# Layer 2's weight preparation moved beside an idle engine, two samples' norms moved into the spectra, and the output stage issued in a listed order

## The chip, the cores and the metric

The kernel runs on one NeuronCore of a Trainium2 chip. Five engines matter: TensorE (PE, matrix products; PEld are its weight loads), VectorE (DVE), ScalarE (ACT), GpSimd (POOL) and SyncE (SP), which here only issues DMA transfers. Each takes its own list of instructions in order and waits on semaphores for the others. The metric is the device time of one execution in microseconds (us). The profile is one execution seen by the hardware profiler.

## The reference, cut to what matters

The input is x of shape (4, 56, 56, 128) in float32. Four layers follow, each as x = x + layer(group_norm(x)):

```python
# layer 0: attention in shifted 7x7 windows, then attention over all 3136 positions, then an MLP
# layer 1: edge features relu(x_i W1 + x_j W2), summed over j; a node matrix
# layer 2: a spectral ("neural operator") attention block over 56x56 images, 128 images a sample
#   xa_n = _inorm(xa, norm_g[0], norm_b[0])
#   k, q, v = _fno_layer(xa_n, wK..), _fno_layer(xa_n, wQ..), _fno_layer(xa_n, wV..)   # FFT products
#   attn_w = softmax(q k^T / sqrt(d)); out = attn_w v
#   projd = _fno_layer(out, wP..); attention = _inorm(projd + xa); an = _inorm(attention)
#   m = _fno_layer(an, wM0.., gelu); m = _fno_layer(m, wM1..); return _inorm(m) + attention
# layer 3: relu of a 3-tap convolution with row and column sums, plus x
```

Three things are concerned here. First, layer 2 needs for each sample the group norm and the image norm of layer 1's result ("norms"), before its Fourier transforms ("spectra"). Second, two tables that depend on the weights alone: one for the scores (from wQ and wK) and one for the values (from wV and wP). Third, everything from the projection to the end ("the output stage").

## The kernel before: the parts that the change and the steps touch

The samples go one after the other through layers 0 and 1. Within a sample the order is 7x7 windows, attention over all positions, MLP, edge layer. The norms of sample b-1 for layer 2 are steps of a generator that the window code of sample b interleaves with its own work (`beside`):

```python
def norms(b, bank):
    if b < 0:
        return iter(())
    return normed_images(k, w2, st, b, io, bank, x1w, xad[b])

for b in range(B):                       # B = 4 samples
    first_layers(lambda *a: fast_attention(*a, functools.partial(norms, b - 1), k.mr[:, b, :]), I["x"][b],
                 x2d[b] if b < B - 1 else None, loaded=b == 0)
```

The norm of one sample, cut (every `yield` ends a step):

```python
def normed_images(k, w, st, b, wk, bank, xp, xad):
    for t in range(HH):                              # HH = 56
        nc.vector.bn_stats(rows[:, t, :], x[:, t, :])
        if t % 2 == 1:
            yield
    nc.vector.bn_aggr(mv, ...)
    ...                # a chain of small DVE operations, four small matmuls and one ACT square root
    for t in range(0, HH, 14):
        apply_norm(k, x[:, t:t + 14, :], x[:, t:t + 14, :], mr)       # DVE, in place
        if t == 42:
            nc.sync.dma_start(xad, x)                # the normed image goes to memory
    ...                # ACT root, DVE reciprocal and scale: st.norm[:, b, 1, :]
```

Between the layers, the images are loaded back, and the spectra stage starts. PE, ACT and DVE follow the order of the program there (`manual_schedule`):

```python
def images(b):
    if b not in loaded:
        xp = loaded[b] = x2p.tile([P, HH + 1, HH], F32, name="s_x2")
        for t in range(0, HH, 28):
            nc.sync.dma_start(xp[:, t:t + 28, :], xad[b, :, t:t + 28, :])
        ...
for b in range(2):
    images(b)
nc.sync.dma_start(x2d[B - 1], x1)
...                                                  # loads of layer 3's and of the convolution weights
with tc.tile_pool(name="g_wk", bufs=1, side="right") as wk:
    all_score_weights(k, I, w2, sp, wk, st)          # POOL alone
    value_weights(k, I, w2, wk, dd)                  # POOL alone
    spectra(k, w2, st, xad, images)

def spectra(k, w, st, xad, images):
    ...
    norm = normed_images(k, w, st, B - 1, wk, ..., st.x1, xad[B - 1])
    first = [first_transform(k, st, b, (wk, psum), st.x1 if b == B - 1 else images(b), zs) for b in range(B)]
    for _ in first[0]:
        pass
    for b in range(B):
        for n, _ in enumerate(sample_spectra(k, st, b, (wk, psum), zs.pop(b))):   # 13 steps
            for _ in range(3):
                next(norm, None)
            if b < B - 1 and n in (2, 5, 7, 9):
                next(first[b + 1])

def first_transform(k, st, b, pools, x, to):         # 4 steps
    for t0 in range(0, HH, 14):
        for t in range(14):
            for ri in range(2):
                nc.tensor.matmul(ps[...], xf[...], k.fw[:, ri, :], start=True, stop=True)   # s_pr
        nc.vector.tensor_mul(z[:, :, t0:t0 + 14], ps..., bc(st.norm[:, b, 1, t0:t0 + 14], 1, 33))
        nc.scalar.copy(z[:, :, HH + t0:...], z[:, :, t0:t0 + 14])
        yield
```

`sample_spectra` takes `z` through further products (`s_ps`, a second `s_pr`, eight groups `s_px`), whose results ACT and DVE copy out. The weight tables are built by some 55 POOL operations of up to 128x512 elements.

The output stage is a plan of 788 operations: 40 for two groups of attended rows and 187 for each sample, two half samples and the last layer. Each is a short group of instructions of one engine, with a list of operations that must come before it and the buffers that it takes and gives back. Before, a list scheduler with estimated costs chose the order:

```python
class Plan:
    HOP, SETS = 0.25, 1.3
    def issue(self):
        while left:
            best = None
            for op in left:
                ...            # the earliest start t by estimated costs, dependences and free buffers
                if t is not None and (best is None or t < best[0] - 1e-9):
                    best = t, op
            op.run()
            free[op.engine] = op.end = t + op.cost
            ...
```

The operations of a half sample follow one chain: `over_h` (PE, 14 matmuls, L1883), `over_c` (PE, L1900), `over_w` (PE, L1914), `product` (PE, L1936), then DVE and POOL combine, ACT squares, `sums` (PE, L1967), a root, and again, three times over. The last layer of a sample has four `convolve` operations (PE, L2317, 12 matmuls each or 6), which need nothing of the other samples.

## Time and profile before

| quantity | value |
|---|---|
| time, median of 3 (lowest, highest) | 3878.21 us (3872.31, 3882.3) |
| span of the profiled execution | 3873.3 us |
| busy share PE, DVE, ACT, POOL | 92%, 75%, 54%, 31% |
| mean granted PE clock | 0.958 |
| spectra: first transform to first score product | 2888.7 to 2977.5 us |
| output stage, after the last mixing products | about 3476 to 3873.3 us |

How to read it: PE is busy nearly everywhere, so the sum of busy times does not say where something can be gained. One goes by stages. A table by stretches of time gives for each stretch its length, each engine's busy time with the number of instructions, and the PE clock that was granted. Where PE is busy for less than the stretch, or its clock is under 1, something other than the number of products sets the time. Waits are read engine by engine: the time that an engine stood idle, and what it stood for.

The four passes through layers 0 and 1 take about 700 us each and are the larger part of the span. Of these, the change touches only the 7x7 windows.

### The profile page before, as it was taken

What the parts mean: (1) busy time and instruction counts of PE and PEld (TensorE: products, weight loads), DVE (VectorE), ACT (ScalarE), POOL (GpSimd) and SP (SyncE); (2) the same over time, 40 slices, a digit from 0 to 9 for tenths busy, and PEclk for the clock granted to TensorE, in tenths of its full rate; (3) what the DMA queues carried; (4) which work ended last, traced back from release to release, by engine and by line L of the source; (5) the groups of instructions that cost most, each with busy time, mean ns of one, the idle gap of its engine ahead of it and who ended that gap; (6) DMA issues with size and microseconds to landing.
All of it is one profiled execution on the core that took longest, in us unless ns stands there. A gap on an engine that the chain in (4) does not pass through costs nothing. (4 is left out here: it accounts for less than half of the span.)

```text
span 3873.3 us, 79430 instructions
## 1 busy us (share of the span) xinstructions
PE 3546.0 (92%) x35416; PEld 1589.1 (41%) x35416; DVE 2897.3 (75%) x2703; ACT 2077.8 (54%) x2080; POOL 1210.6 (31%) x667
## 2 busy tenths in 40 slices
PE   6899999989998998999989989999998989989988
PEld 4422234543322455322245532223456433336654
DVE  6588877859887786688869758887776767765664
ACT  4577765448776554677745457776542012214332
POOL 0000006600000570000028300000655769975555
PEclk8999999999999999999999999999998989998888
DMA  2000000000000000000000000000011058831101
GB/s 96 1 1 1 1 1 19 19 18 1 1 1 1 18 3 34 1 1 1 1 17 3 19 18 1 1 1 34 2 44 49 1 121 170 175 101 59 52 8 50
DMA packets 73496, 111.12 MB, mean 29 GB/s; under 512 B 62140, under 2 KB 63932, under 8 KB 67900
## 3 DMA queue, kind: packets, MB, share of 16 engines
q1 hardware_dynamic: 14460, 93.13, 8.0%
q10 hardware_dynamic: 58688, 12.85, 2.0%
q8 instruction: 279, 4.57, 0.5%
q14 instruction: 69, 0.57, 0.0%
HBM read 79.46 MB, written 26.51 MB: 27 GB/s over the span
## 5 line engine op out<-in xcount | busy, mean ns | idle before, releaser
L663 ACT ACTIVATE f_ring<-f_s 128x1792 f32<-128x1792 f32 (+3 forms) x796 | 1097.3, 1429 | 226.6 <-PE f_s L661 224.8
L606 DVE TENSOR_TENSOR f_acc<-f_acc,f_ring 128x1792 f32<-128x1792 f32 x560 | 1134.1, 2025 | 64.3 <-ACT f_ring L663 7.5
L661 PE MATMUL f_s<-f_qT,f_kT 32*128 32x448 f32 x5376 | 738.3, 572 | 47.9 <-ACT f_ring L663 27.9
L877 POOL TENSOR_TENSOR m_sq<-m_y 128x392 f32<-128x392 f32 x16 | 14.5, 919 | 1975.4 <-ACT m_y L876 1975.3
L612 PE MATMUL f_po<-f_ring,f_va 128*32 128x448 f32 x5376 | 589.8, 546 | 0.0
L1029 DVE TENSOR_TENSOR e_td<-e_pa,e_c 128x1792 f32<-128x1792 f32 x252 | 491.3, 2013 | 14.4 <-ACT e_a L994 14.4
L1031 POOL TENSOR_TENSOR e_tp<-e_a,e_c 128x1792 f32<-128x1792 f32 x140 | 451.8, 3257 | 145.1 <-PE e_acc L1036 104.4
L661 PEld LDWEIGHTS f_s<-f_qT,f_kT 32*128 32x128 f32 x5376 | 268.4, 183 | 524.5 <-ACT f_ring L663 378.9
L1036 PE MATMUL e_acc<-e_td,t_shared 32*32 32x448 f32 x8064 | 323.7, 546 | 22.0 <-DVE e_td L1029 10.9
L1033 ACT ACTIVATE e_tp<-e_tp 128x1792 f32<-128x1792 f32 x140 | 235.1, 1696 | 176.2 <-POOL e_tp L1031 176.2
L1645 DVE TENSOR_TENSOR u_ud<-u_px,u_d 112x1792 f32<-112x1792 f32 x144 | 240.1, 1708 | 96.4 <-PE u_po L1650 87.3
L612 PEld LDWEIGHTS f_po<-f_ring,f_va 128*32 128x32 f32 x5376 | 133.2, 109 | 396.3 <-issue 395.3
L1036 PE MATMUL e_acc<-e_tp,t_shared 32*32 32x448 f32 x4480 | 222.3, 547 | 3.2 <-ACT e_tp L1033 2.5
L1650 PE MATMUL u_po<-u_ud,AT 112*64 112x448 f32 x960 | 201.6, 550 | 23.3 <-DVE u_ud L1645 23.3
L1647 POOL TENSOR_TENSOR u_up<-xh,u_d 112x1792 f32<-112x1792 f32 x64 | 193.8, 3054 | 25.7 <-PE u_po L1650 12.4
L1036 PEld LDWEIGHTS e_acc<-e_td,t_shared 32*32 32x32 f32 x8064 | 134.1, 103 | 146.4 <-DVE e_td L1029 56.0
L629 DVE RECIPROCAL f_den<-f_den 128x448 f32<-128x448 f32 x28 | 82.7, 2953 | 77.2 <-ACT f_den L628 77.2
L1650 PE MATMUL u_po<-u_up,AT 112*64 112x448 f32 x576 | 126.9, 548 | 0.2
L1650 PEld LDWEIGHTS u_po<-u_ud,AT 112*64 112x64 f32 x960 | 64.9, 137 | 147.9 <-issue 86.7
L606 DVE TENSOR_TENSOR f_acc<-f_ring 128x1792 f32<-128x1792 f32 x28 | 56.7, 2025 | 86.6 <-ACT f_ring L663 57.7
L1512 POOL TENSOR_TENSOR q_u<-iS,q_g 128x1792 f32<-128x1792 f32 x32 | 102.7, 3237 | 56.2 <-PE s_px L1360 33.4
L1036 PEld LDWEIGHTS e_acc<-e_tp,t_shared 32*32 32x32 f32 x4480 | 95.2, 103 | 55.3 <-ACT e_tp L1033 19.4
(485 smaller groups left out, 4797.0 us busy)
## 6 DMA issues: line engine op xcount, KB each, us to landing
u_d<-dd SPq DMA_DIRECT2D x48, 784.0 KB
xw<-in_x SPq DMA_DIRECT2D x4, 1568.0 KB
x2d<-x SPq DMA_DIRECT2D x4, 1568.0 KB
xad<-x SPq DMA_DIRECT2D x4, 1568.0 KB
x_xs<-xad ACTq DMA_DIRECT2D x32, 196.0 KB
xm<-x_ev ACTq DMA_DIRECT2D x64, 98.0 KB
o_a<-xm SPq DMA_DIRECT2D x8, 784.0 KB
o_x<-x2d SPq DMA_DIRECT2D x4, 1568.0 KB
```

What stands on the lines that cost most here:

```text
L606: nc.vector.tensor_add(acc, slots(j, 0) if c == 1 else acc, slots(j, c))
L612: nc.tensor.matmul(po[heads[h], :NB], va[o, c, heads[h]], p, start=(c == 0), stop=(c == 24))
L661: nc.tensor.matmul(ss[:, i, :NB], kT[heads[h], c * P:(c + 1) * P], qT[heads[h], blk(j)], start=True, stop=True)
L663: nc.scalar.activation(ring[:, slot:slot + m, :], ss[:, :m, :NB], AF.Exp, scale=scale)
L1029: nc.vector.tensor_tensor(t, am, cm, ALU.max)
L1031: nc.gpsimd.tensor_sub(t, bc(a.rearrange("p (l n) -> p l n", l=8), 1, 4), cm)
L1033: nc.scalar.activation(tf, tf, AF.Relu)
L1036: nc.tensor.matmul(acc[quarters[q], r, :NB], k.ident[o, o], t[o, q].rearrange("p l n -> p (l n)"), start=(g == 0), stop=(g == len(EDGE_TUR ...
L1512: nc.gpsimd.tensor_mul(u, bc(st.iS[:, bp, c, :HH], 1, HEADS), bc(g[:, n, c, :], 2, HH))
L1645: nc.vector.tensor_mul(u, bc(px[:, :, :NB], 2, m), dm)
L1647: nc.gpsimd.tensor_mul(u, bc(x, 2, m), dm)
L1650: nc.tensor.matmul(po[64 * b2:64 * b2 + 64, :NB], st.AT[:, 8 * i + h0 + q, 2 * bp + b2, :], u[:, b2, q, :], start=(left == 16), stop=(left ...
```

## The change

It has two parts. The first moves work between stages:

- The weight tables of layer 2 are built beside sample 0's 7x7 windows, where POOL has only memsets to do. Their results go to memory (`gd`, `dd`), and `g` is loaded back before the spectra.
- Only sample 0's norms stay beside windows (the windows of sample 1). The norms of samples 1 and 2 move from the windows of samples 2 and 3 into the spectra, where before only sample 3's norms were. The spectra take the samples in the order 0, 3, 1, 2, and load samples 1 and 2 as they came from layer 1 (`x2d`), not normed (`xad`).

```diff
@@ spectra
-        norm = normed_images(k, w, st, B - 1, wk, ..., st.x1, xad[B - 1])
+        order = [0, B - 1, *range(1, B - 1)]
+        def steps(n):
+            for norm in norms[:1]:
+                for _ in range(n):
+                    if next(norm, norm) is norm:
+                        norms.pop(0)
+                        break
+        norms = [normed_images(k, w, st, b, wk, ..., of(b), xad[b]) for b in order[1:]]
...
         for _ in first[0]:
-            pass
-        for b in range(B):
+            steps(3)
+        for i, b in enumerate(order):
             for n, _ in enumerate(sample_spectra(k, st, b, (wk, psum), zs.pop(b))):
-                for _ in range(3):
-                    next(norm, None)
-                if b < B - 1 and n in (2, 5, 7, 9):
-                    next(first[b + 1])
+                if i < B - 1 and 8 <= n < 12:
+                    while n == 8 and len(norms) + i >= B - 1:
+                        steps(1)
+                    next(first[i + 1])
+                steps(4)
@@ all_score_weights
-    st.g = pool.tile([P, 2, 16, HEADS], F32, name="q_g")
-    st.g4 = pool.tile([P, 2, 1, HEADS], F32, name="q_g4")
+    g = wk.tile([P, 2, 17, HEADS], F32, name="q_g")
...
+    nc.sync.dma_start(gd, g)
@@ value_weights
-    nc.gpsimd.tensor_copy(f[:, 0], d[:, 0])
...                      # the three results are written from d and w.V, without the copy
@@ build
+            def layer2_weights():
+                ...      # all_score_weights(.., gd), then value_weights(.., dd)
             def norms(b, bank):
-                if b < 0:
+                if b == 0:
+                    layer2_weights()
+                if b != 1:
                     return iter(())
-                return normed_images(k, w2, st, b, io, bank, x1w, xad[b])
+                return normed_images(k, w2, st, 0, io, bank, x1w, xad[0])
...
-                    nc.sync.dma_start(xp[:, t:t + 28, :], xad[b, :, t:t + 28, :])
+                    nc.sync.dma_start(xp[:, t:t + 28, :], (x2d if b else xad)[b, :, t:t + 28, :])
...
+                g = sp.tile([P, 2, 17, HEADS], F32, name="g")
+                nc.sync.dma_start(g, gd)
+                st.g, st.g4 = g[:, :, :16], g[:, :, 16:]
+                spectra(k, w2, st, xad, images)
```

The second part replaces the list scheduler of the output stage by a fixed list of the 788 operations, which a search has found. The operations, their dependences and their buffers are the same:

```diff
-    def issue(self):
-        ...              # list scheduling by estimated costs
+    def issue(self, order):
+        assert sorted(order) == list(range(len(self.ops)))
+        ...
+        for n in order:
+            op = self.ops[n]
+            ...
+            op.run()
...
+OUTPUT_ORDER = """
+0 40 119 227 306 10 3 2 1 4 5 13 12 11 14 15 6 9 7 8 18 19 16 17 41 228 120 42 307 121 43 45 44 122 124 229 47
...
+781 782 785 786 787
+"""
-        plan.issue()
+        plan.issue([int(n) for n in OUTPUT_ORDER.split()])
```

## The prediction, as it was put on record before the run

> **What bounds the kernel now.** I read the page first: PE 92% busy, clock 0.958, so the average shows no single spare place and one has to go by stages. Next a table by stretches: the 7x7 windows of the four samples, the spectra, the output stage. (Columns: length; busy us and instructions of PE, PEld, DVE, ACT, POOL; granted PE clock; DMA share; GB/s.)

> ```profile
> 55.20:155.10 99.90, 91.01 (x728) 55.65 (x728) 52.61 (x100) 47.64 (x80) 6.85 (x18) 0.94 0.00 1
> 755.10:865.00 109.90, 94.77 (x732) 57.13 (x732) 66.52 (x181) 48.12 (x82) 6.80 (x18) 0.92 0.07 28
> 1465.10:1575.00 109.90, 94.76 (x732) 57.12 (x733) 66.51 (x181) 48.14 (x82) 6.79 (x18) 0.92 0.07 28
> 2178.50:2288.40 109.90, 94.85 (x732) 57.24 (x732) 66.60 (x181) 48.13 (x82) 6.86 (x18) 0.92 0.07 28
> 2888.50:2977.50 89.00, 73.31 (x1208) 64.04 (x1208) 50.70 (x133) 32.94 (x72) 39.24 (x58) 0.88 0.28 97
> 3476.00:3873.30 397.30, 353.89 (x2202) 233.34 (x2200) 225.47 (x393) 144.65 (x203) 221.45 (x132) 0.85 0.12 45
> ```

> Sample 0's windows carry no norm and take 99.9 us; the others carry one and take 109.9. So a norm beside windows costs 10.0 us, though DVE is far from full: its operations stand in DVE's queue ahead of the copies that PE waits for.

> In the spectra POOL's weight tables run beside sample 3's norm. DVE's timeline shows operations on one element per partition that take over 1 us next to others of 0.15:

> ```profile
> 2917.72 0.15 DVE L1764 TENSOR_TENSOR factors<-factors,t_w_ms 128x1 f32<-128x1 f32 x1
> 2918.51 0.94 DVE L1255 TENSOR_TENSOR s_t<-s_mv,s_mr 128x1 f32<-128x1 f32 x1
> 2919.49 1.18 DVE L1256 SCALAR_TENSOR_TENSOR s_t<-s_t,s_mv 128x1 f32<-128x1 f32 x1
> 2930.58 4.62 DVE L193 TENSOR_SCALAR x<-x,s_mr 128x784 f32<-128x784 f32 x4
> ```

> PE's timeline of the same stretch, in brackets the idle time and what ended it:

> ```profile
> 2912.17 0.38 PE L1250 MATMUL s_pt<-s_mv,t_shared 128*128 128x1 f32 x2 [3.49 <-DVE s_mv L1247]
> 2920.73 0.58 PE L1259 MATMUL s_pt<-s_t,t_shared 128*128 128x1 f32 x2 [3.83 <-DVE s_t L1256]
> 2926.20 0.68 PE L1283 MATMUL s_pt<-s_mean,c_ones_c 128*128 128x56 f32 x2 [1.72 <-DVE s_mean L1279]
> 2929.73 0.67 PE L1292 MATMUL s_pt<-s_sq,c_ones_px 128*128 128x56 f32 x2 [2.43 <-DVE s_sq L1289]
> ```

> From 2908 to 2933 PE does little, waiting for one norm; after it a sample takes 16.6 us (2933.3, 2950.0, 2966.6), bound by PE. In the output stage PE is busy 353.9 of 397.3 us at a clock of 0.85: idle time and clock cost about 43 and, at 15% of 354, some 53 us. Its waits have many causes and no main one:

> ```profile
> PE o_b L1967 <- ACT o_t L1956: 9.1, 4, 6.5
> PE o_d L1900 <- POOL o_v L2159: 6.3, 4, 3.6
> PE o_b L1967 <- ACT o_sq L2019: 3.9, 1, 3.9
> PE o_d L1883 <- ACT o_y L2034: 2.9, 1, 2.9
> ```

> [...] L1256 took 1.18 us beside POOL operations of 1.2 us, 0.22 us beside an idle POOL; the scaling of a 128x784 piece took 1.15 us against 0.68. [...]

> **The change, part by part.**

> *a. Windows of samples 2 and 3.* They lose their norms: 2 x (109.9 - 99.9) = 20.0 us off a path on which nothing else is parallel. **-20.**

> *b. Windows of sample 0.* They gain about 50 POOL operations, in the spectra some 33 us of POOL. Their loads (1.2 MB) begin near 53 us, when memory is idle; at the 420 GB/s that the image loads reached they need 3 us and are there before POOL ends its memsets at 62. Up to 16 normalisations wait on average half a POOL operation, 0.6 us, two groups ahead of use. I put **+1**.

> *c. Start of the spectra.* Before, SP issued the image loads at 2673, long ahead. In the built program after, the load of `g` stands before them on SP and waits for the edge layer's last matmul, since its buffer lies where the edge layer works (e_td). The images then wait too. From 2887.6: issue and start 1.2 us, `g` (0.56 MB) 1.3, the first image (1.6 MB) 3.8 at 420 GB/s, of which half must be there: first product near 2893 instead of 2888.7, **+4.5**. DVE loses it as well, its first operation being the copy-out.

> *d. First norm in the spectra (sample 3).* Its chain, from the aggregate to the norm, took 24.3 us (2912.1 to 2936.4). Without POOL I take off 7 us of excess in the chain and 5.5 in the convolution-weight operations (L1750 to L1768) between: about 12 to 15. **-10.**

> *e. Two more norms in the spectra.* In the program's order a sample is: four rounds of first transform and `s_px` (1.82 + 0.97 us on PE, so 11 us), with 24 `bn_stats` hidden beside; then 32 more at 0.123 us (3.9), the aggregate 1.67, and the chain: operations 8.7 us, four trips to PE and one to ACT 3. PE starts on the first scaled quarter, about 2 us before the chain ends. Sum 11 + 3.9 + 1.7 + 11.7 - 2 = 26.3 us a sample against 16.6. Twice: +19.4. The first sample's own 32 odd `bn_stats`, of which before 30 lay beside products, and PE at a lower clock in these gaps add some 9. **+28.**

> Spectra: 4.5 - 10 + 28 = about +23. First part: -20 + 1 + 23 = **+4**.

> *f. Output stage.* Same operations, same buffers, so only idle time and clock can change. I compared both orders on PE. A PE operation that needs the result of an earlier PE operation through another engine, with no other PE operation between, stands still for the whole detour; there are 12 such pairs before and 4 after (with at most one between: 33 and 29). Before, sample 3 ends with half 1 alone: nine of the twelve lie among PE's operations 155 to 185, and there the trace has 3.65, 3.91, 1.44, 1.33 and 1.28 us of idle PE. After, both halves of sample 3 alternate to the end, and the last layer's means stand before sample 2's last convolve. Some 8 detours of 2 us are filled: -16. What stays: the first product waits for the attended rows (2.87 us), the end after the last product (some 7 us). The clock should gain a few us, and a list found for estimated durations loses a few on the chip. **-18, between -45 and +5.**

> Sum: 3878.2 - 20 + 1 + 23 - 18 = **3864 us**.

> **The rivals.** *Spectra costs nothing.* If the norms fill PE's gaps, as the step counts intend, the stage stays near 89 us. For it: DVE was busy only 50.7 us there, and the POOL contention goes. Against it: the norm is a chain, a sample's first product needs its end, and three chains now follow one another with PE starved. Then the time would be near 3842. *POOL's tables disturb sample 0's windows.* If DVE's small operations there suffer as in the spectra (7 us in a chain of 24), sample 0 loses 5 to 10 us: 3870. [...] *The order yields nothing.* PE was 89% busy in the output stage, and the clock, not the idle time, may be the larger loss; a different mixture of small matmuls can lower it. Then 3880 to 3890. *The order yields much.* If the filled gaps also keep the clock at 0.92, 7% of 354 us come on top: 3840.

> **Range and chances.** The two parts nearly cancel in my sum and each has an error of about 15 us; together some 22. The range is 3834 to 3894. For 2% the time must fall under 3800.6 or rise over 3955.8. The first needs the favourable rival in the spectra and 45 us from the order; the second has no mechanism that I can see. Faster 0.03, within 2% 0.95, slower 0.02.

> **What would show it.** a: windows of samples 2 and 3 at 100 us. b: sample 0's at 101, POOL busy from 62 to about 100 us. c: PE idle for 4 to 5 us after the edge layer's last product, ended by a DMA. d: L1256 at 0.2 us and the 128x784 scalings at 0.7. e: the spectra at 105 to 115 us, three gaps of about 12 us in which PE waits for DVE's s_mv, s_t, s_mean and s_sq. f: output stage at 375 to 385 us, with fewer idle gaps after 3800. The prediction is wrong if the spectra stay under 95 us, or if the output stage changes by over 45 us or by nothing.

## The result, and the profile after

The changed kernel takes 3833.43 us (median of 4 runs, 3827.72 to 3834.5) against 3878.43 us (4 runs, 3872.31 to 3882.3): 0.9882 of the time, 95% interval 0.9865 to 0.9900. Predicted were 3864 us and a range of 3834 to 3894, so the sum was -14 where -45 was measured. Two lines of the profiled run's page (its span is 3825.9 us):

```profile
PE 3515.6 (92%) x35416; PEld 1573.8 (41%) x35416; DVE 2884.8 (75%) x2703; ACT 2078.0 (54%) x2080; POOL 1209.1 (32%) x666
PEclk9999999999999999999999999999997989999999
```

TensorE is busy for 92% of the span as before, with as many instructions, but for 3515.6 us instead of 3546.0. The same work became shorter. (The trace holds two MATMUL records for each product: the 28 products of one round of the first transform stand as x56.) The row of granted clocks is lowest at its 7, a slice that lies in the spectra. The table by stretches has the same six stages as before, in the same order (sample 0's to 3's windows, spectra, output stage):

```profile
52.40:150.60 98.20, 89.47 (x724) 55.17 (x724) 52.95 (x100) 47.57 (x80) 40.45 (x69) 0.96 0.09 33
752.20:862.90 110.70, 96.56 (x736) 58.98 (x736) 66.86 (x181) 48.17 (x82) 6.81 (x18) 0.89 0.07 28
1462.80:1560.20 97.40, 88.51 (x724) 55.00 (x725) 51.87 (x100) 47.74 (x80) 6.87 (x18) 0.96 0.04 16
2163.80:2262.00 98.20, 88.30 (x724) 55.10 (x725) 51.89 (x100) 47.74 (x80) 6.87 (x18) 0.97 0.04 16
2862.30:2985.50 123.20, 94.22 (x1224) 82.21 (x1224) 67.96 (x295) 34.43 (x76) 3.45 (x5) 0.76 0.28 104
3479.30:3825.90 346.60, 320.94 (x2232) 209.79 (x2232) 225.99 (x396) 145.36 (x207) 221.57 (x133) 0.96 0.15 56
```

Measured from the edge layer's last product and from the first row product, so that both kernels are cut at the same instructions, the balance of the two profiled runs (3873.3 and 3825.9 us) is this:

| stage | before | after | difference | predicted |
|---|---|---|---|---|
| windows, samples 2 and 3 | 219.8 | 195.6 | -24.2 | -20 |
| windows, sample 0 (tables beside) | 99.9 | 98.2 | -1.7 | +1 |
| spectra | 89.8 | 124.4 | +34.5 | +23 |
| scores and mixing | 493.9 | 493.8 | 0 | 0 |
| output stage | 401.8 | 346.6 | -55.3 | -18 |

The rows add up to -46.7 of the -47.4 us between the two spans. The -1.7 of sample 0 is not an effect of the tables: see b below.

The output stage's gain splits in two: idle TensorE fell from 44.2 to 25.6 us (-18.6), and busy TensorE from 357.6 to 320.9 us (-36.7) at a clock of 0.96 instead of 0.85. The idle part is what the prediction said. The clock part it had put at "a few us". In the spectra the clock went the other way, from 0.89 to 0.76. TensorE's timeline there (start, length, product, in brackets the idle time before it):

```profile
2867.85 6.84 PE L1322 MATMUL s_pr<-t_images,s_x 128*64 128x33 f32 x145 [6.67 <-DMA s_x<-xad]
2894.85 3.20 PE L1322 MATMUL s_pr<-t_images,x 128*64 128x33 f32 x56
2931.78 1.83 PE L1322 MATMUL s_pr<-t_images,s_x 128*64 128x33 f32 x56
2962.01 1.83 PE L1322 MATMUL s_pr<-t_images,s_x 128*64 128x33 f32 x56
```

The last three lines are the first round of three successive samples, 36.9 and 30.2 us apart. The same 28 products take 3.20 us in the first and 1.83 in the others: half clock. Two lines of VectorE's timeline answer to term d:

```profile
2886.18 0.22 DVE L1256 SCALAR_TENSOR_TENSOR s_t<-s_t,s_mv 128x1 f32<-128x1 f32 x1
2893.72 2.47 DVE L193 TENSOR_SCALAR x<-x,s_mr 128x784 f32<-128x784 f32 x4
```

Without GpSimd beside it the small operation takes 0.22 us (1.18 before) and the four scalings 2.47 us (4.62 before).

### The profile page after: what moved, and what is told of

Read it like the earlier page. It is cut to its first block, busy times and chain, and to the rows that moved or that the text cites. A ratio compares the mean times of both kernels' runs of the same rounds, so it can differ in the third digit from the quotient of the medians.

```text
span 3825.9 us, 79457 instructions
## 1 busy us (share of the span) xinstructions
PE 3515.6 (92%) x35416; PEld 1573.8 (41%) x35416; DVE 2884.8 (75%) x2703; ACT 2078.0 (54%) x2080; POOL 1209.1 (32%) x666
## 5 line engine op out<-in xcount | busy, mean ns | idle before, releaser
L1529 POOL TENSOR_TENSOR q_u<-iS,g 128x1792 f32<-128x1792 f32 x32 | 102.8, 3238 | 126.6 <-PE s_px L1360 103.7
L1036 PEld LDWEIGHTS e_acc<-e_tp,t_shared 32*32 32x32 f32 x4480 | 94.6, 103 | 55.2 <-ACT e_tp L1033 19.4
```

The costliest lines, as they stand in the source:

```text
L1036: nc.tensor.matmul(acc[quarters[q], r, :NB], k.ident[o, o], t[o, q].rearrange("p l n -> p (l n)"), start=(g == 0), stop=(g == len(EDGE_TUR ...
```

## The experiments

Two questions: do the parts add up, and what sets the clock? For the second the theories changed on the way.

### The two parts alone

**order_only** is the kernel before with the listed order in the output stage; **first_only** is the changed kernel with the old list scheduler there.

```diff
- plan.issue()                     # order_only: new line in the old kernel
+ plan.issue([int(n) for n in OUTPUT_ORDER.split()])
- plan.issue([int(n) for n in OUTPUT_ORDER.split()])   # first_only: the reverse
+ plan.issue()
```

> The kernel before with the new order in its output stage and nothing else. If the two parts of the change are independent and the output stage's 55 us come from the order alone: 3878 - 55 = 3823 us, faster than the changed kernel, output stage near 347 us at a clock near 0.96. If the gain needs the new first part too (what is in flight, or what the clock has seen, when the output stage begins): between 3840 and 3870, with the output stage's clock still under 0.92.

> The changed kernel with the old list scheduler in its output stage: the new first part alone. If the parts add up: windows -26 in all, spectra +34, start of the program -3, so 3878 to 3888 us, output stage near 400 us at a clock near 0.85. If the first part helps the output stage's clock: under 3860.

order_only: 3821.44 us, 0.9851 (0.9834 to 0.9868). first_only: 3887.44 us, 1.0023 (1.0009 to 1.0036). The order alone gives all the gain and more; the first part costs about 11 us between the medians. They add up: -55 + 11 = -44. order_only's output stage, in the table by stretches:

```profile
3472.44:3819.60 347.16, 322.39 (x2232) 210.50 (x2232) 226.07 (x396) 145.30 (x207) 221.72 (x133) 0.96 0.15 56
```

The 0.96 comes from the order, whatever ran before it: in the seven traces that have the new order and nothing added to it, the stage takes 346.2 to 347.5 us. The old order is less steady. Its stage took 401.8 us in the kernel before and 412.7 in first_only, whose ten runs spread from 3874.99 to 3896.7 us (the profiled one is the slowest). So the cost of the first part is known to some 10 us only; by the balance above, windows and spectra alone come to about +9.

### The first part taken apart

**tables_early** keeps the tables beside sample 0 and puts the norms of samples 0 to 2 back into the windows. **g_apart** only moves the load of `g`.

```diff
  def norms(b, bank):              # tables_early
      if b == 0:
          layer2_weights()
-     if b != 1:
          return iter(())
-     return normed_images(k, w2, st, 0, io, bank, x1w, xad[0])
+     return normed_images(k, w2, st, b - 1, io, bank, x1w, xad[b - 1])
  ...                              # tables_early: spectra() as in the kernel before
- nc.sync.dma_start(g, gd)         # g_apart, and in tables_early too
+ nc.scalar.dma_start(g, gd)
```

> The changed kernel with the weight tables beside sample 0's windows and the new order kept, but the norms of samples 0 to 2 back in the windows of samples 1 to 3; only sample 3's norm stays in the spectra, and the load of g goes from ScalarE's queue. If the two added norms are what made the spectra 34 us longer, and the absent tables what made its one norm shorter: windows of samples 1 to 3 at 110 us each, spectra 75 to 80 us, 3805 to 3812 us in all, the fastest of all. If a norm's chain costs the spectra the same with or without the tables beside it: spectra 88 us, 3820 us.

> The changed kernel with the load of g on ScalarE's queue, so that the image loads no longer stand behind it. If that load is what PE waits 6.7 us for at the start of the spectra: that gap gone, spectra 116 to 118 us, 3826 to 3829 us. If the images wait for something else (their data, their buffers): the gap stays and the time is 3833.

tables_early: 3825.95 us, 0.9860 (0.9841 to 0.9878), spectra 96.7 us. g_apart: 3838.31 us, 0.9897 (0.9880 to 0.9913), spectra 128.7 us. Both expectations missed. In both traces SyncE issued the image loads only 12 to 13 us before their use (at 2879.4 and 2851.7 us), though no load of `g` stood ahead of them. I read the reason in the built program: the loads wait for a count of GpSimd's instructions. The branch that isn't taken ends with the weight tables, which use the memory where the images go, and the count to wait for is that of the later of both branches. In the branch taken GpSimd reaches it only in the edge layer. To try this, **images_early** and **norms_back** compute the tables ahead of the loop in the branch that is not taken:

```diff
  with small.Else():
+     layer2_weights()
      with tc.For_i(0, B, 1) as b: ...
-     layer2_weights()
```

images_early is g_apart with this, norms_back is tables_early with this and with `g` loaded after `spectra(...)` in the program's order.

> The changed kernel with the load of g on ScalarE's queue and, in the branch that does not run, the weight tables computed before the loop instead of after it, so that the image loads can be issued near 2670 us as before and not 10 us ahead of their use. If the start of the spectra is lost to the late image loads: no DMA wait at its start, spectra 110 to 116 us, 3821 to 3827 us. If the three norm chains alone make the length: 120 us, 3831 us.

> Weight tables beside sample 0's windows, norms of samples 0 to 2 back in the windows of samples 1 to 3, new order, and both the image loads issued early (tables ahead of the loop in the branch that does not run) and the load of g after the first sample. If late image loads took the gain in the run with early tables: spectra 78 to 84 us, 3807 to 3813 us, fastest so far. If the norm of sample 3 costs the same with no tables beside it: spectra 88 us or more, 3818 us or more.

The loads then went out at 2650 us in images_early and at 2675 in norms_back. The first load of g_apart and of images_early, whose programs differ in nothing but the place of that one line:

```profile
2851.68 1.97 SPq L2553 DMA_DIRECT2D s_x<-xad  x2
2649.69 0.80 SPq L2553 DMA_DIRECT2D s_x<-xad  x2
```

images_early: 3831.02 us, 0.9899 (0.9881 to 0.9918), spectra 123.9 us, no better than the changed kernel. norms_back: 3815.39 us, 0.9843 (0.9820 to 0.9866), spectra 83.6 us, a little less gain than expected. TensorE at the start of images_early's spectra:

```profile
2864.98 0.68 PE L1322 MATMUL s_pr<-t_images,s_x 128*64 128x33 f32 x17 [1.00 <-DVE x L1009]
2867.43 5.64 PE L1322 MATMUL s_pr<-t_images,s_x 128*64 128x33 f32 x128 [1.76 <-issue]
2873.91 4.48 PE L1322 MATMUL s_pr<-t_images,s_x 128*64 128x33 f32 x79 [0.85 <-issue]
```

The wait for the images is gone, but two gaps in which TensorE waits for nothing that shows ("issue") stand in its place, beside DMA engines that are full (share 1.00 from 2865 to 2870 us) with `g`, the store of sample 3 and the convolution's weights. What held TensorE in them was not shown. Idle TensorE at this start fell from 7.9 us in the changed kernel (6.67 + 1.24) to 3.6. Behind the gaps 79 records take 4.48 us, half clock again, and the stage's clock is 0.72 instead of 0.76: what the early loads gained, the clock took.

### What sets the clock: idle time is not enough

My first theory was that short idle gaps start the half-clock stretches. **filled_old** and **filled_new** put small dummy matmuls (64 columns, to spare PSUM columns) on TensorE ahead of the operations that wait, in the old and in the new order.

```diff
+ if op.at in FILL: self.fill(FILL[op.at])
  op.run()
+ def fill(n):
+     for _ in range(n):
+         k.nc.tensor.matmul(plan.spare[:, NB:], k.g4, k.ident[:, :64], start=True, stop=True)
```

> The kernel before, old order, with 166 small dummy matmuls (64 columns of the identity, written to spare PSUM columns that nobody reads) queued on TensorE ahead of those 22 operations of the output stage that wait 0.3 us or longer; about 25 us of the idle time is filled with work, and no real work starts sooner. If idle gaps are what starts the half-clock stretches: output stage's clock from 0.85 to 0.93 or more, 3840 to 3860 us. If the old mixture and order of the small products sets the clock: clock still near 0.85, 3876 to 3890 us.

> The kernel before with the new order, and 57 dummy matmuls ahead of the 14 operations that still wait there. If gaps start the half-clock stretches: output stage's clock from 0.96 to 0.98 or more, 2 to 8 us less than the 3821 us of the order alone. If not: 3821 us or a few more.

filled_old: 3910.88 us, 1.0098 (1.0082 to 1.0115). filled_new: 3838.39 us, 0.9926 (0.9902 to 0.9950), 17 us slower than the order alone: its output stage went from a clock of 0.96 to one of 0.93. Idle time in filled_old's output stage fell to 29.0 us, and the clock did not rise (0.85 before):

```profile
3475.73:3914.60 438.87, 409.91 (x2564) 289.54 (x2564) 228.47 (x396) 146.31 (x207) 221.83 (x132) 0.84 0.12 45
```

So the theory fell. The clock in steps of 1 us gave the next one: stretches of half clock last whole multiples of 3.41 us (3.4 to 23.9 us in the kernel before, but for one that the end of the span cuts), and all changes of the clock lie on one grid of 3.41 us within a run, in the kernel before to within 0.01 us. Here is one start in the kernel before, in windows of that grid (columns as in the table by stretches: the number after the length is busy TensorE, the third from the end its clock), and TensorE's timeline below:

```profile
3537.91:3541.32 3.41, 3.41 (x38) 3.39 (x38) 1.58 (x4) 0.62 (x2) 2.22 (x2) 0.99 0.00 0
3541.32:3544.73 3.41, 3.41 (x22) 2.59 (x20) 0.39 (x1) 2.48 (x3) 3.33 (x2) 0.50 0.00 0
3554.97:3558.40 3.43, 3.43 (x28) 1.60 (x26) 2.33 (x3) 0.00 (x0) 0.27 (x1) 1.00 0.02 5
```

```profile
3537.98 1.06 PE L1994 MATMUL o_b<-o_r,slot 128*128 128x14 f32 x8
3538.90 4.08 PE L1914 MATMUL o_d<-t_images,o_t 128*128 128x64 f32 x28
3543.82 6.24 PE L1914 MATMUL o_d<-t_images,o_t 128*128 128x64 f32 x28
3553.05 4.17 PE L1936 MATMUL o_d<-o_z,t_images 56*112 56x448 f32 x16
```

TensorE has not a moment of idle time in the window from 3537.91, and yet the clock halves after it (the windows shown lie some 0.07 us late on the grid, hence 0.99). What it does there is thin: products of 14 and of 64 columns, each behind a weight load of 128. The clock comes back after a window with 448-column products.

I then counted, for each 3.41-us window, how much of the array was used: for every MATMUL record columns x 0.86 ns (two records of 448 columns make the 0.77 us that a product lasts at full clock) x its share of 128 rows and of 128 weight columns (the largest product in these traces is 128*128), both rounded up to 32, spread evenly over the record. The rounding and the weights are choices of mine. This is my count from the traces, not a view of the profile. It takes the output stages of eleven runs (those of the runs below included) and the changed kernel's spectra:

```
array used in the window   windows   followed by the full clock
under 0.30                 149         5
0.30 to 0.36                57         0
0.36 to 0.40                41         5
0.40 to 0.44                46        33
0.44 to 0.50               125       125
0.50 and over              833       833
```

One threshold at 0.42 puts 1221 of 1251 windows right; columns alone, without rows and weight columns, get at most 1147, idle time alone at most 1059. In the stretch above the shares of five successive windows are 0.36 (ahead of the drop), 0.29, 0.26, 0.34 and 0.47, and the full clock follows the last. Idle time itself decides nothing: 91 windows had none and a share under 0.38, and 90 of them were followed by half clock; 34 had over 1 us idle and a share of 0.44 or more, and all were followed by the full one. The count ties the order to the clock: 34 of the 117 windows of the output stage lie under 0.42 in the kernel before, and 9 of 101 in order_only. By this count it also follows why stretches are long: at half clock the same products fill less of a window (one round of the changed kernel's spectra 0.32, against 0.57 at the full clock), so what held the full clock there did not bring it back.

The number is fitted to these stages. Over the first 3476 us of the kernel before, which the count did not use, 0.42 puts 991 of 1014 windows right. All 931 windows at or above it were followed by the full clock; the 23 misses lie below it, 18 of them between 0.36 and 0.42. There columns alone do about as well (1001, with a threshold of 0.49), so how rows and weight columns are to be weighed stays open.

### The rule put to the test: more work, less time

If this is right, added work can make the kernel faster. **dense_old** is the kernel before plus 17 matmuls that fill the array (0.77 us each), their places chosen by laying the operations' lengths and gaps from the trace against the rule, so that thin windows come over the threshold. **thin_old** has three 14-column products in place of each. **dense_elsewhere** has the same 17 ahead of the last layer's 448-column products, where the count finds the array well used anyway.

```diff
+ def dense(k, ps, times, n=NB):             # thin_old: three times as many, n=14
+     for _ in range(times):
+         k.nc.tensor.matmul(ps[:, :n], k.gw[:, 0, :], k.wide[:, :n], start=True, stop=True)
+ FILL = {761: 1, 177: 1, 548: 1, 748: 1, 743: 2, 729: 2, 109: 1, 387: 1, 42: 2, 198: 2, 44: 1, 271: 1, 670: 1}   # other keys in dense_elsewhere
- return psum.tile([P, 512], F32, tag="b", name="o_b", bufs=2)
+ return plan.filled(psum.tile([P, 512], F32, tag="b", name="o_b", bufs=2))   # dense() into the bank first
```

> The kernel before, old order, with 17 added dummy matmuls that fill the whole array (128x128 weights, 448 columns, 0.77 us each at the full clock), written to the bank of the operation that follows and overwritten by it, ahead of 13 operations of the output stage where the array is thinly used. Nothing real is removed. Theory (the traces so far): the clock is set anew every 3.41 us, to half where the array was used for less than 40% of it in the 3.41 us before, whether by idle time or by products with few columns. Then half-clock time falls from 117 us to some 20 to 50, and added work makes the kernel faster: 3835 to 3860 us. If the clock has another cause: 13 us of added work, of which half in gaps, 3875 to 3890 us.

> The same places and about the same time on TensorE, but with three products of 14 columns (about 0.25 us each) in place of each full one, so that TensorE is as busy and the array nearly unused. Array-use theory: no gain, clock 0.85 or lower, 3880 to 3900 us. If being busy is what keeps the clock: the same time as the run with full dummies.

> The same 17 full dummy matmuls as in the run that placed them where the array is thinly used, but ahead of the last layer's 448-column products, where the array is well used anyway. Array-use theory: half-clock time stays near 117 us, the clock near 0.85, and the dummies cost what they last, 3880 to 3892 us. If any added work, or any shift of the stage against the 3.41 us grid, gains some 10 us, as the thin dummies seemed to: 3860 to 3870 us.

dense_old: 3852.45 us, 0.9934 (0.9917 to 0.9951), 24 us faster with 17 products more. dense_elsewhere: 3886.99 us, 1.0029 (1.0020 to 1.0039), 10 us slower with the same 17. Both lie where the theory put them. thin_old: 3866.51 us, 0.9976 (0.9959 to 0.9993). The output stages of dense_old and dense_elsewhere, each from its own trace:

```profile
3478.36:3851.70 373.34, 338.28 (x2266) 217.16 (x2266) 228.99 (x396) 146.74 (x207) 221.62 (x132) 0.95 0.14 52
```

```profile
3472.94:3885.70 412.76, 367.64 (x2266) 239.90 (x2266) 226.92 (x396) 146.83 (x207) 221.57 (x132) 0.87 0.12 47
```

Half-clock time in the stage is 37 us in dense_old, 111 in dense_elsewhere and 117 in the kernel before. Same work added, opposite sign: the place decides. thin_old missed its expectation: its stage took 391.5 us, with 90 us at half clock, where I expected no fewer than 117. Window by window the rule held there too, but for three windows. Why it fell on the good side stays open; its 10 us are no more than the old order's stage varies without any edit (401.8 and 412.7 us), while dense_old's 28 us in the stage (373.3) are.

**dense_spectra** and **dense_all** use the rule. In the norm, full dummies stand where TensorE waits for the chain; dense_spectra has them on images_early, dense_all on norms_back, with ten more in the new order.

```diff
  ps = bank()
+ dense(k, ps, fill[0])        # fill = (4, 0, 2, 1) in dense_spectra, (3, 0, 1, 1) in dense_all
  nc.tensor.matmul(ps[:, 0:1], k.g4, mv[:, 0:1], start=True, stop=True)
```

> The changed kernel with early image loads (the run of that name, 3831 us, spectra 124 us at a clock of 0.72), and in each of its three norms seven full dummy matmuls put where TensorE waits for the norm's chain (four before the mean's product, two and one before the two last). Array-use theory: clock in the spectra over 0.85, spectra 106 to 114 us, 3813 to 3822 us. If the chains themselves are the length: spectra 120 us or more, 3830 us or more.

> The fastest so far (tables early, norms of samples 0 to 2 in the windows, new order, early image loads: 3815 us) with five full dummies in sample 3's norm and ten in the output stage, where the new order still leaves 26 us at half clock. Array-use theory: 3800 to 3809 us. Otherwise 3815 to 3825 us.

dense_spectra: 3819.09 us, 0.9847 (0.9830 to 0.9863), 12 us less than images_early; spectra 112.6 us at a clock of 0.89, where images_early has 123.9 at 0.72. Its dummies (L1808) in one chain, and the first rounds of the samples:

```profile
2897.59 1.82 PE L1329 MATMUL s_pr<-t_images,x 128*64 128x33 f32 x56
...
2924.71 1.83 PE L1329 MATMUL s_pr<-t_images,s_x 128*64 128x33 f32 x56
...
2937.19 3.17 PE L1808 MATMUL s_pt<-t_images 128*128 128x448 f32 x8
2940.94 0.38 PE L1254 MATMUL s_pt<-s_mv,t_shared 128*128 128x1 f32 x2 [0.58 <-DVE s_mv L1250]
...
2951.70 1.83 PE L1329 MATMUL s_pr<-t_images,s_x 128*64 128x33 f32 x56
```

The first rounds are now 27.1 and 27.0 us apart, where they are 38.2 and 30.3 in images_early (36.9 and 30.2 in the changed kernel), and none takes 3.20 us. dense_all is the fastest of all: 3803.63 us (3801.5 to 3807.16), 0.9811 (0.9795 to 0.9827). Both lie in the range that the theory gave. dense_all's spectra and output stage:

```profile
2888.96:2966.73 77.77, 71.44 (x1219) 61.13 (x1219) 39.26 (x134) 32.93 (x72) 4.22 (x6) 0.99 0.23 82
3462.05:3805.30 343.25, 321.81 (x2252) 208.08 (x2252) 225.95 (x396) 145.32 (x207) 221.84 (x133) 0.98 0.15 57
```

## Why the prediction was right and wrong

**f, the output stage: the step that failed.** Its working, that "only idle time and clock can change", was right, and so was the idle term: -16 put, -18.6 measured. The mis-sized term is "The clock should gain a few us": it was -36.7. I had read the clock of 0.85 as 53 us to be had at most, and then treated it as a by-product of the idle time. The runs show it as a quantity of its own, which followed what lay together within 3.41 us (in 1221 of the 1251 windows counted). The stage changed by 55 us, more than the 45 that the prediction itself had named as a sign of being wrong. The rival "The order yields much" named the mechanism, a clock kept at 0.92, and put 3840; I gave it too little weight, although the profile showed a clock of 0.97 in the scores and mixing, so that more was plainly to be had. "The order yields nothing" fell with order_only.

**e, two more norms: right at the full clock, too small at the granted one.** The chain of 26.3 us a sample was measured as 27.0 and 27.1 where dummies held the clock, and as 36.9 and 30.2 where nothing did. The prediction allowed some 9 us for odd `bn_stats` and "PE at a lower clock in these gaps" together (the clock was 0.58 from 2910 to 2930 us in the kernel before); the two chains alone took 14.5 us more than twice the 26.3. What it missed is that the four rounds which started at half clock did not bring the full clock back: in the first of the three samples each of the four took 3.20 us. A round (3.20 us and the 1.84 us of the eight records beside it, 4.9 us together) fills 0.32 of the array at half clock by the count above, under 0.42; at full clock (1.83 and 1.04 us, 2.73 together) it fills 0.57, and the rounds of the later samples, which started at full clock, kept it.

**c, start of the spectra: +4.5 put, a gap of 6.67 us and one of 1.24 measured.** (The terms that the prediction lists add up to 4.4 us, which gives 2892.0 and +3.3, unless the issue is counted twice.) The images did wait, ended by a DMA as foreseen. The cause named was a part of it: SyncE issued `g` at 2861.3 us and the images right behind it, at 2861.8. Without the load of `g` ahead of them the image loads went out at 2851.7 us, and TensorE's wait for them fell from 6.67 to 3.18 us; the rest was the wait for the branch that isn't taken: in images_early no DMA wait is left there. In g_apart a gap of 4.83 us without a releaser took the place of what was saved; with both waits removed, smaller gaps of that kind and the half clock took the gain.

**a: -20 put, -24.2 measured.** The norm's removal also raised the windows' clock from 0.92 to 0.96 and 0.97. The prediction had taken sample 0's 99.9 us as the length without a norm; the two windows took 97.4 and 98.2.

**b: +1 put, -1.7 measured.** The gain is not the tables' doing. order_only, where they are not beside these windows, has the same length:

```profile
52.20:150.40 98.20, 89.47 (x726) 55.22 (x726) 52.48 (x100) 47.63 (x80) 6.83 (x18) 0.96 0.00 1
```

So with equal clock the tables cost 0 us: GpSimd is busy for 40.45 us instead of 6.83 and VectorE for 52.95 instead of 52.48. Why they added only 0.47 us to VectorE here, where in the spectra its small operation took 1.18 us beside GpSimd, was not shown. The rival "POOL's tables disturb sample 0's windows" fell.

**d: the operations right, the saving put too high.** Both operation lengths came out as put. In norms_back, where only the tables moved, the spectra fell from 90.1 us (order_only) to 83.6: -6.5, of the -10 put. The stage varies without any edit to it (89.7 to 96.7 us in the traces with the old first part), but always above 83.6. "Spectra costs nothing" fell as well: with three norms in it the stage took 112.6 to 128.7 us in all five traces.

**The range.** The two large errors are of one kind, the clock, and of opposite sign: it gave 37 us in the output stage and took some 11 in the spectra (123.9 us in images_early against 112.6 with dummies). That they partly cancelled, and left the time only 0.6 us below the range, is luck. An error of 15 us for each part left out that a tenth of the clock on 350 us of products is 35 us.

## What to carry to other kernels

Read the clock by stage, and where it is low look 3.4 us ahead of each drop (in these traces the use of the array in that window told the clock of the next one 1221 times in 1251): not for idle time alone, but for products with few columns, rows or weight columns that stand together. For another kernel, the grid and the threshold have to be read from its own traces. Reordering so that thin products and waits lie between full ones can be worth more than the waits it fills (here 36.7 us of busy time beside 18.6 of idle time), and a full dummy product in an unavoidable wait may pay for itself, as it did here in dense_old (24 us), dense_spectra (12 us less than images_early) and dense_all (12 us less than norms_back). A step moved to a stage where TensorE already waits can cost its length at a lowered clock: 36.9 and 30.2 us a sample here, against 27.1 and 27.0 where dummies held it.
